# A selective-scan kernel: the list order of layer 1's scans is made again with other durations and priorities

## The chip, the cores and the metric

The kernel runs on one core of one Trainium2 chip. The metric is the device time of one execution in microseconds (us). The core has five engines that run side by side, each working through its own instructions strictly in order: TensorE (PE in the profile; its weight loads are listed apart as PEld), VectorE (DVE), ScalarE (ACT), GpSimd (POOL) and SyncE (SP), which here only issues DMAs. An instruction that must wait for another engine holds up everything behind it on its own engine.

## The reference, cut to what matters

Two layers follow each other. Layer 0 works on four images of 128x128 positions and 192 channels. Layer 1, which the change touches, runs a selective scan in four directions over the same positions, with 16 states for each channel:

```python
proj = einsum('kbcl,kcd->kbld', xs, x_proj_w)          # dpart (12), B (16), C (16)
delta = softplus(einsum('kblr,krc->kblc', dpart, dt_w) + 2 * dt_b)
def step(state, inp):
    d, b, c, uu = inp
    dA = exp(d[..., None] * A_neg)                     # A_neg = -exp(A_logs)
    state = dA * state + (d * uu)[..., None] * b[:, :, None, :]
    y = einsum('kbcn,kbn->kbc', state, c)
    return state, y
```

The four directions' y, plus Ds * xs, are added; a layer norm, a gate and an output projection follow, outside of the change.

## The kernel before, in words

The stages run one after the other: transposing the input, layer 0, layer 1's projection and convolution (in_conv), layer 1's scans (scans), and the outputs. Only the scans are changed. All data is float32.

**Tiling.** The four images make two pairs, and two pairs times four directions times 16 chunks of 1024 positions make 128 steps. In a step lie 6 tiles, each of 64 channels of one image. A tile's 128 partitions hold 64 channels times two halves of the 16 states, so that it takes 8 units, one for each state of a half. Below, "tile 3" is the fourth of its step, and a "unit" is one state pair of a tile. For each unit:

- ACT makes dA = exp(delta * A) into one of two PSUM buffers (exp, L1201).
- DVE scans over 1024 positions, in place in the buffer h (scan, L1207).
- POOL multiplies by C into one of three buffers hc (product, L1213).
- PE sums the two state halves into Y (sum, L1221, two matmuls of 512 columns).

What the scan of a tile starts from is delta * u * B, spread over 8 slots of h. It comes from 8 fills: PE multiplies transposed delta*u by diagonals that carry B (fill, L1174: 8 matmuls on 32-row tiles) into the single PSUM buffer f, and ACT copies it into h (evict, L1185). Each of a tile's 8 evictions writes into all 8 of its slots. So a tile's first scan needs all 8 fills, and there are as many fills as units: 48 in a step. h has 18 slots, so a tile's first eviction waits until the sixth unit of the tile two before it is through its product.

After a tile's 8 sums, DVE adds Y to what earlier directions left (add, L1243, L1247 or L1249, by the direction). Y has one PSUM buffer, so the next tile's first sum waits for this add.

**Preparation of the next step.** While a step's tiles 3 to 5 run, the next step is prepared, and every part of it goes through one PSUM bank, s: two projections (L1028, three matmuls each, copied by ACT, L1034); six step-size matmuls (L1051), each followed by a softplus on ACT (L1054); delta*u on POOL (L1061, three in a step); six groups of four transposes (L1070), copied by ACT or DVE (L1076); eight diagonal matmuls (L1094), each spread by DVE (L1100). As the bank is single, a preparing matmul waits for the engine that empties the bank from the one before. Softplus and exp need different ACT tables: each change between them is an ACT_TABLE_LOAD.

**What sets the order.** Nothing above is emitted where it is written. op() records an operation with its engine, an assumed duration in us, what it reads and writes, and a priority: its place in the list less `early`. Order.emit() then plays the list through: it takes, of all operations whose inputs and buffers are free, the one with the smallest key. The key is the engine's free time for all operations that could start within `idle` of it, and then the priority; a change of ACT table adds `keep` to the rank. What comes out is one fixed instruction order for each engine, the DMA queue of SP among them. The durations decide the order, and nothing else: on the chip the semaphores make each instruction wait for what it really needs.

Of the kernel before, what the change touches and what calls it, by code (L numbers as in the profile page):

```python
# [12 lines left out]
ALU = mybir.AluOpType  # L13
# [187 lines left out]
class Maker:  # L201
# [741 lines left out]
    def scans(self, xc, delta, cs, y, w, ident, alog, dsum, dtb2):  # L943
# [10 lines left out]
        nc, tc = self.nc, self.tc  # L954
# [11 lines left out]
        with ExitStack() as ctx:  # L966
# [9 lines left out]
            for q in (2, 3):  # L976
                nc.vector.tensor_tensor(mask, mask, ident[:, 32 * q : 32 * q + 32], ALU.add)

            od = Order(window=3000, keep=1047, idle=0.500, rate=265e3)
            op = od.op  # L980

            def buf(tag, bufs, *shape, pool=p1, stream=None):
# [5 lines left out]
            us, pj, wts, dT, D, C, dd, h, st, prev, Y = ({} for _ in range(11))  # L988
# [15 lines left out]
            def load_u(s):  # L1004
                p, k, at, j = steps[s]
                for i in range(3):
                    t = us[s, i] = buf("u", 3, 128, T)
                    op("SP", 0.1, lambda t=t, i=i: nc.sync.dma_start(
                        t(), xc[k // 2][p][i][:, j * T : (j + 1) * T]
                    ), writes=[t], size=524e3, early=192)  # L1010
                if at == 0:
                    wt = buf("w", 2, 128, 2, 3, 128)
                    op("SP", 0.2, lambda: [
                        nc.sync.dma_start(wt()[:, 0], w["xp1"][:, k]),
                        nc.sync.dma_start(wt()[:, 1], w["dtw1"][:, k]),
                    ], writes=[wt], size=393e3, early=90)
                    wts[p, k] = wt

            def project(s):
                p, k, _, j = steps[s]  # L1020
                wt, uu = wts[p, k], [us[s, i] for i in range(3)]
                t = pj[s] = buf("pj", 1, 128, T)
                for c in range(2):
                    g = bank("P")

                    def mm(g=g, c=c):
                        for i in range(3):
                            nc.tensor.matmul(  # L1028
                                g(), wt()[:, 0, i], uu[i]()[:, 512 * c : 512 * c + 512],
                                start=(i == 0), stop=(i == 2),  # L1030
                            )

                    op("PE", 2.65, mm, reads=[wt, *uu], writes=[g], claims=[t])
                    op("ACT", 0.59, lambda g=g, c=c: nc.scalar.copy(  # L1034
                        t()[:, 512 * c : 512 * c + 512], g()), reads=[g, t], writes=[(t, c)])

                def store():
                    for e in range(2):
                        r = 64 * e + DR + NS
                        nc.sync.dma_start(cs[2 * p + e][k][:, j * T : (j + 1) * T], t()[r : r + NS])  # L1040

                op("SP", 0.2, store, reads=[(t, 0), (t, 1), t], writes=[("cs", s)], size=131e3)

            def step_sizes(s, i):

                p, k, _, j = steps[s]
                wt, u, x = wts[p, k], us[s, i], pj[s]
                l = buf("l", 3, 128, T)
                for c in range(2):
                    g = bank("P")  # L1050
                    op("PE", 0.9, lambda g=g, c=c: nc.tensor.matmul(  # L1051
                        g(), wt()[:, 1, i], x()[:, 512 * c : 512 * c + 512], start=True, stop=True,
                    ), reads=[wt, (x, c), x], writes=[g], claims=[l], early=-123)
                    op("ACT", 0.6, lambda g=g, c=c: nc.scalar.activation(  # L1054
                        l()[:, 512 * c : 512 * c + 512], g(), AF.Softplus,
                        bias=dtb2[:, i % 2, k : k + 1],
                    ), reads=[g], writes=[l], table="softplus")
                op("SP", 0.1, lambda: nc.sync.dma_start(
                    delta[p][i][k][:, j * T : (j + 1) * T], l()
                ), reads=[l], writes=[("delta", s, i)], size=524e3)  # L1060
                op("POOL", 2.4, lambda: nc.gpsimd.tensor_tensor(u(), l(), u(), ALU.mult),  # L1061
                   reads=[l], writes=[u], early=30)
                t = dT[s, i] = buf("dT", 4, 128, 2, 8, 64)
                for c in range(2):
                    g = bank("P")

                    def mm(g=g, c=c):
                        for q in range(4):
                            b = 512 * c + 128 * q
                            nc.tensor.transpose(  # L1070
                                g()[:, 128 * q : 128 * q + 128], u()[:, b : b + 128], ident
                            )

                    op("PE", 0.95, mm, reads=[u], writes=[g], claims=[t], early=-249)
                    def turn(copy, g=g, c=c):
                        copy(  # L1076
                            t()[:, :, 4 * c : 4 * c + 4],
                            g().rearrange("t (q h c) -> t h q c", h=2, c=64),
                        )

                    if i < 2:
                        op("ACT", 0.6, lambda turn=turn: turn(nc.scalar.copy), reads=[g], writes=[t], early=-579)
                    else:
                        op("DVE", 0.69, lambda turn=turn: turn(nc.vector.tensor_copy),
                           reads=[g], writes=[t], early=-180)

            def diagonals(s, e, sb):
                x, t, g = pj[s], buf("D", 5, 128, 2, 512), bank("D")
                r = 64 * e + DR

                def mm():
                    for a in range(2):
                        b = 256 * sb + 128 * a
                        nc.tensor.matmul(  # L1094
                            g()[:, NS * a : NS * a + NS], x()[:, b : b + 128], ident[:, r : r + NS],
                            start=True, stop=True,
                        )

                def spread():
                    nc.vector.tensor_tensor(  # L1100
                        t().rearrange("t a (n s) -> t (a n) s", s=32),
                        g()[:, : 2 * NS].unsqueeze(2).to_broadcast([128, 2 * NS, 32]),
                        mask.unsqueeze(1).to_broadcast([128, 2 * NS, 32]),
                        ALU.mult,
                    )

                op("PE", 0.4, mm, reads=[(x, sb // 2), x], writes=[g], claims=[t], early=-105)
                op("DVE", 1.2, spread, reads=[g], writes=[t], early=15)
                D[s, e, sb] = t


# [48 lines left out]
            def fill(m, sb, rp):  # L1160

                s, x = divmod(m, 6)
# [3 lines left out]
                td, tD = dT[s, i], D[s, e, sb]  # L1166
                gs = buf("f", 1, 128, 2, 512, pool=psF)
# [10 lines left out]
                                    start=True, stop=True,  # L1178
                                )

                op("PE", 1.12, mm, reads=[td, tD], writes=[gs], claims=h[m])

                def evict():
                    for at, q, nq in runs(m):
# [4 lines left out]
                            gs().rearrange("p n (a q s) -> p q a n s", a=2, s=32)[:, q : q + nq],  # L1189
                        )  # L1190

                op("ACT", 1.13, evict, reads=[gs], writes=h[m])

            def unit(m, q):
                p, k, at, j, x, e, hf, i, r = info(m)
                hq, d, tC = h[m][q], dd[m], C[m // 3, q]
                hs = H[:, (NQ * m + q) % SLOTS]
                a, t = buf("dA", 2, 128, T, pool=psA), buf("hc", 3, 128, T)
                c = (hf * 4 + k) * NQ + q
                way = slice(None) if k % 2 == 0 else slice(None, None, -1)  # L1200
                op("ACT", 1.16, lambda: nc.scalar.activation(  # L1201
                    a(), d(), AF.Exp, scale=alog[:, c : c + 1]),
                    reads=[d], writes=[a], table="exp", early=-522)
                s0 = st.get((x, m - 6))

                def scan():
# [2 lines left out]
                        0.0 if at == 0 else s0()[:, q : q + 1], ALU.mult, ALU.add,  # L1209
                    )  # L1210

                op("DVE", 2.34, scan, reads=[a, *([s0] if at else [])], writes=[hq])
                op("POOL", 2.4, lambda: nc.gpsimd.tensor_tensor(t(), hs, tC(), ALU.mult),  # L1213
                   reads=[hq, tC], writes=[t])
                if q == 0:
                    Y[m] = buf("Y", 1, 128, 512, pool=psY)
                ym = Y[m]
# [5 lines left out]
                            start=(q == 0), stop=(q == NQ - 1),  # L1223
                        )

                op("PE", 0.95, sum_n, reads=[t], writes=[ym], early=-252)

            def finish(m):
                p, k, at, j, x, e, hf, i, r = info(m)
                ym, t = Y[m], buf("y", 2, 128, 512)  # L1230
                if at < NCH - 1:
                    sm = st[x, m] = buf(f"st{x}", 2, 128, NQ)
                    last = T - 1 if k % 2 == 0 else 0

                    def keep():
                        for a, q, nq in runs(m):
                            nc.scalar.copy(sm()[:, q : q + nq], H[:, a : a + nq, last])  # L1237

                    op("ACT", 0.22, keep, reads=h[m], writes=[sm])

                def add():
                    if k == 0:
# [9 lines left out]
                    for th, a in enumerate(y_part(y[k // 2][p][i], m)):  # L1252
                        nc.sync.dma_start(a, t()[64 * th : 64 * th + 64])

                op("DVE", 0.72, add, reads=[ym, *([prev[m]] if k != 2 else [])], writes=[t])
                op("SP", 0.2, store, reads=[t], writes=[("y", p, k // 2, j, x)], size=262e3)

            FILLS = [(sb, rp) for sb in range(4) for rp in range(2)]
# [403 lines left out]
```

## Time and profile before

| | us |
|---|---|
| median of 3 runs | 26409.49 |
| lowest and highest run | 26333.76 and 26457.49 |
| the profiled execution | 26512.26 |
| its span, first to last instruction | 26510.5 |
| of it, the scans (first to last eviction and product), 7180 to 24910 | 17730 |
| PE busy in the scans | 16270.53 |
| DVE busy in the scans | 15700.51 |
| POOL busy in the scans | 15212.16 |
| ACT busy in the scans | 14689.00 |
| granted TensorE clock in the scans | 0.94 |

The profiled execution is 102.8 us (0.4%) above the median of the runs, and some 2 us longer than its span. A busy share is the time in which at least one instruction of an engine was running. The granted clock is the share of full speed that TensorE was given: 1.00 is full, and 0.94 a mean over stretches at full and at half speed. In the waits view a row names the engine and line that waited, whom for, the total, how often, and the longest. In the timeline a bracket at the end of a row gives the idle time of the engine before the instruction and what ended it.

### The profile page before, as it was taken

The numbers are of one execution on the slowest core, as the hardware profiler recorded it, in microseconds if no ns is written. First come the engines' busy times: TensorE is split into PE (matmuls) and PEld (weight loads), VectorE is DVE, ScalarE is ACT, GpSimd is POOL, SyncE is SP. The second block draws the span as 40 slices with busy tenths as digits, with TensorE's granted clock in tenths as the row PEclk, the third lists the DMA queues.
The fourth block names the chain that finished last, engine by engine and source line by source line (L and its number), as shares of the span: only waits on it lengthen the run. The fifth ranks groups of instructions, "written<-read, shape, count | busy, mean of one in ns | idle before, by whom it ended". The sixth has DMA issues, their size and how long they took to land.

```text
span 26510.5 us, 438073 instructions
## 1 busy us (share of the span) xinstructions
PE 24193.3 (91%) x169220; PEld 9017.9 (34%) x169220; DVE 21935.4 (83%) x15401; ACT 21016.8 (79%) x24359; POOL 19902.8 (75%) x9450
## 2 busy tenths in 40 slices
PE   5999999998799999999999999999999999999699
PEld 3333333332233333333333333333333333333255
DVE  4888888888788889989898888888898888988643
ACT  5988898985588888888888888888888888888433
POOL 3777777763488888888888888888888888888400
PEclk7999999998899999999999899999899999999799
DMA  7999999995544444444444444444444444444573
GB/s 213 242 239 241 242 239 241 239 241 182 185 130 127 133 130 136 135 128 125 117 126 134 126 135 130 130 130 130 125 136 131 117 123 115 133 130 130 182 236 105
DMA packets 1667058, 4220.17 MB, mean 159 GB/s; under 512 B 238545, under 2 KB 387473, under 8 KB 1661905
## 3 DMA queue, kind: packets, MB, share of 16 engines
q1 hardware_dynamic: 1664976, 4192.14, 58.0%
q8 instruction: 1340, 21.95, 0.4%
q14 instruction: 742, 6.07, 0.1%
HBM read 3252.11 MB, written 939.10 MB: 158 GB/s over the span
## 4 chain that ended last, share of the span: by engine, by line
PE 40%; DVE 18%; ACT 11%; issue 6%; DMA 4%; POOL 3%; SPq 0%; DVEq 0%; POOLq 0%; ACTq 0%
DVE h L1207 14%; PE f L1174 13%; PE Y L1221 11%; ACT h L1185 6%; PE s L1028 3%; ACT dA L1201 3%; POOL hc L1213 2%; PE s L1051 2%; DMA C<-cs 2%; PE z L785 1%; PE hf L574 1%; DVE D L1100 1%; DVE acc L896 1%; PE f L785 1%; PE s L1094 1%
## 5 line engine op out<-in xcount | busy, mean ns | idle before, releaser
L1213 POOL TENSOR_TENSOR hc<-h,C 128x1024 f32<-128x1024 f32 x6144 | 14335.4, 2362 | 2412.5 <-PE Y L1221 1154.9
L1207 DVE TENSOR_TENSOR_SCAN h<-dA,st,h 128x1024 f32<-128x1024 f32 x5760 | 13130.9, 2331 | 779.9 <-ACT st L1237 290.6
L1185 ACT COPY h<-f 128x1024 f32<-128x1024 f32 (+3 forms) x8192 | 6332.9, 799 | 2256.1 <-PE f L1174 2185.0
L1174 PE MATMUL f<-D,dT 32*64 32x256 f32 x98304 | 7167.9, 408 | 777.5 <-ACT h L1185 633.6
L1221 PE MATMUL Y<-hc,sel 128*64 128x512 f32 x24576 | 7001.5, 657 | 475.1 <-POOL hc L1213 219.9
L1201 ACT ACTIVATE dA<-d,alog 128x1024 f32<-128x1024 f32 x6144 | 6905.9, 1124 | 301.6 <-DVE h L1207 247.2
L1174 PEld LDWEIGHTS f<-D,dT 32*64 32x64 f32 x98304 | 3279.1, 138 | 6688.2 <-ACT h L1185 4815.8
L452 POOL TENSOR_TENSOR xs<-xs,pr 128x1024 f32<-128x1024 f32 x1536 | 3637.3, 2371 | 329.2 <-ACT pr L447 249.4
L595 DVE SCALAR_TENSOR_TENSOR hf<-hh,vec,hf 128x512 f32<-128x512 f32 x3072 | 2317.8, 755 | 412.9 <-PE hf L574 272.7
L1221 PEld LDWEIGHTS Y<-hc,sel 128*64 128x64 f32 x24576 | 1322.6, 141 | 2979.6 <-issue 1811.3
L574 PE MATMUL hf<-sa,diag 96*32 96x512 f32 x18432 | 2152.3, 600 | 13.2 <-DMA sa<-hpad 11.3
L447 ACT ACTIVATE pr<-xi,vec 128x1024 f32<-128x1024 f32 x1536 | 1713.8, 1143 | 301.1 <-POOL xs L452 296.0
L1100 DVE TENSOR_TENSOR D<-s,mask 128x1024 f32<-128x1024 f32 x1024 | 1238.3, 1209 | 842.0 <-PE s L1094 842.0
L534 POOL TENSOR_TENSOR dl<-dl,xs 128x1024 f32<-128x1024 f32 x192 | 454.7, 2368 | 830.6 <-ACT dA L532 735.5
L574 PEld LDWEIGHTS hf<-sa,diag 96*32 96x32 f32 x18432 | 561.9, 109 | 1479.3 <-issue 1390.5
L1061 POOL TENSOR_TENSOR u<-l,u 128x1024 f32<-128x1024 f32 x384 | 907.2, 2363 | 163.4 <-ACT l L1054 136.0
L1207 DVE TENSOR_TENSOR_SCAN h<-dA,h 128x1024 f32<-128x1024 f32 x384 | 857.1, 2274 | 78.5 <-ACT dA L1201 45.3
L1051 PE MATMUL s<-pj,w 128*128 128x512 f32 x1536 | 892.3, 664 | 7.0 <-ACT l L1054 2.8
L1028 PE MATMUL s<-u,w 128*128 128x512 f32 x1536 | 756.4, 630 | 53.3 <-DMA prev<-xc 52.6
L1054 ACT ACTIVATE l<-s,vec 128x512 f32<-128x512 f32 x768 | 527.8, 687 | 328.5 <-PE s L1051 323.9
L1094 PEld LDWEIGHTS s<-ident,pj 128*128 128x128 f32 x4096 | 554.1, 196 | 599.5 <-issue 256.7
L392 PE MATMUL f<-xa,w 96*128 96x512 f32 (+1 forms) x1536 | 724.8, 616 | 25.7 <-ACT xi L407 25.5
(202 smaller groups left out, 21859.5 us busy)
## 6 DMA issues: line engine op xcount, KB each, us to landing
C<-cs SPq DMA_DIRECT2D x4096, 256.0 KB, 4.7
sa<-hpad SPq DMA_DIRECT2D x2304, 276.0 KB, 7.1
d<-delta SPq DMA_DIRECT2D x1536, 256.0 KB, 4.1
u<-xc SPq DMA_DIRECT2D x384, 512.0 KB, 4.6
delta<-l SPq DMA_DIRECT2D x384, 512.0 KB, 3.6
y<-y SPq DMA_DIRECT2D x1536, 128.0 KB, 3.2
hh<-hpad SPq DMA_DIRECT2D x384, 414.0 KB, 7.7
hpad<-hp SPq DMA_DIRECT2D x192, 552.0 KB, 7.2
```

Source lines behind the costliest of these rows:

```text
L447: op("ACT", 1.1, lambda pr=pr, t=t: nc.scalar.activation(rows(pr()), x()[:, t // 3 : t // 3 + R, t % 3 : t % 3 + W], AF.Copy, scale=v(k, V ...
L452: op("POOL", 2.38, lambda pr=pr: nc.gpsimd.tensor_tensor(o(), o(), pr(), ALU.add), reads=[pr], writes=[o], early=-429)
L574: nc.tensor.matmul(o()[32 * g : 32 * g + 32], diag[:, d, s, k, g], x[:, g, :, c0 : c0 + W], start=(d == 0 and s == 0), stop=(d == 1 and s ...
L595: nc.vector.scalar_tensor_tensor(o3, hh()[:, 1 + dy : 5 + dy, PAD + dx : PAD + dx + W], v(k, V0_K + col), o3, ALU.mult, ALU.add,)
L1028: nc.tensor.matmul(g(), wt()[:, 0, i], uu[i]()[:, 512 * c : 512 * c + 512], start=(i == 0), stop=(i == 2),)
L1100: nc.vector.tensor_tensor(t().rearrange("t a (n s) -> t (a n) s", s=32), g()[:, : 2 * NS].unsqueeze(2).to_broadcast([128, 2 * NS, 32]), ma ...
L1174: nc.tensor.matmul(gs()[64 * jn : 64 * jn + 64, n, 256 * a : 256 * a + 256], td()[rt, r // 64, 2 * sb + a], tD()[rt, a, 256 * jn : 256 * j ...
L1185: nc.scalar.copy(H[:, at : at + nq, 256 * sb : 256 * sb + 256].rearrange("p q (a r s) -> p q a r s", a=2, s=32)[:, :, :, 2 * rp : 2 * rp + 2],
L1201: op("ACT", 1.16, lambda: nc.scalar.activation(a(), d(), AF.Exp, scale=alog[:, c : c + 1]), reads=[d], writes=[a], table="exp", early=-522)
L1207: nc.vector.tensor_tensor_scan(hs[:, way], a()[:, way], hs[:, way], 0.0 if at == 0 else s0()[:, q : q + 1], ALU.mult, ALU.add,)
L1213: op("POOL", 2.4, lambda: nc.gpsimd.tensor_tensor(t(), hs, tC(), ALU.mult), reads=[hq, tC], writes=[t])
L1221: nc.tensor.matmul(ym()[64 * th : 64 * th + 64], sel, t()[:, 512 * th : 512 * th + 512], start=(q == 0), stop=(q == NQ - 1),)
```

## The change

No operation is added or removed. The list of 49,432 operations of the scans, what each reads and writes, and all buffers are the same; the assumed durations, the priorities and three settings of the planner differ, and with them the order of the instructions. The diff, without its context:

```diff
-            od = Order(window=3000, keep=1047, idle=0.500, rate=265e3)
+            od = Order(window=3000, keep=937, idle=0.400, rate=265e3)
 # load_u: u, weights
-                    ), writes=[t], size=524e3, early=192)
+                    ), writes=[t], size=524e3)
-                    ], writes=[wt], size=393e3, early=90)
+                    ], writes=[wt], size=393e3)
 # project
-                    op("PE", 2.65, mm, reads=[wt, *uu], writes=[g], claims=[t])
+                    op("PE", 2.65, mm, reads=[wt, *uu], writes=[g], claims=[t], early=-219)
-                        t()[:, 512 * c : 512 * c + 512], g()), reads=[g, t], writes=[(t, c)])
+                        t()[:, 512 * c : 512 * c + 512], g()), reads=[g, t], writes=[(t, c)], early=96)
 # step_sizes: matmul, softplus, delta*u, transposes, copies by ACT and by DVE
-                    op("PE", 0.9, lambda g=g, c=c: nc.tensor.matmul(
+                    op("PE", 1.1, lambda g=g, c=c: nc.tensor.matmul(
-                    ), reads=[wt, (x, c), x], writes=[g], claims=[l], early=-123)
-                    op("ACT", 0.6, lambda g=g, c=c: nc.scalar.activation(
+                    ), reads=[wt, (x, c), x], writes=[g], claims=[l])
+                    op("ACT", 0.69, lambda g=g, c=c: nc.scalar.activation(
-                op("POOL", 2.4, lambda: nc.gpsimd.tensor_tensor(u(), l(), u(), ALU.mult),
-                   reads=[l], writes=[u], early=30)
+                op("POOL", 2.38, lambda: nc.gpsimd.tensor_tensor(u(), l(), u(), ALU.mult),
+                   reads=[l], writes=[u])
-                    op("PE", 0.95, mm, reads=[u], writes=[g], claims=[t], early=-249)
+                    op("PE", 1.16, mm, reads=[u], writes=[g], claims=[t], early=-201)
-                        op("ACT", 0.6, lambda turn=turn: turn(nc.scalar.copy), reads=[g], writes=[t], early=-579)
+                        op("ACT", 0.6, lambda turn=turn: turn(nc.scalar.copy), reads=[g], writes=[t], early=9)
-                           reads=[g], writes=[t], early=-180)
+                           reads=[g], writes=[t], early=-96)
 # diagonals: matmul, spread
-                op("PE", 0.4, mm, reads=[(x, sb // 2), x], writes=[g], claims=[t], early=-105)
-                op("DVE", 1.2, spread, reads=[g], writes=[t], early=15)
+                op("PE", 0.4, mm, reads=[(x, sb // 2), x], writes=[g], claims=[t], early=-180)
+                op("DVE", 1.2, spread, reads=[g], writes=[t], early=930)
 # fill, evict
-                op("PE", 1.12, mm, reads=[td, tD], writes=[gs], claims=h[m])
+                op("PE", 1.1, mm, reads=[td, tD], writes=[gs], claims=h[m])
-                op("ACT", 1.13, evict, reads=[gs], writes=h[m])
+                op("ACT", 1.05, evict, reads=[gs], writes=h[m], early=1074)
 # unit: exp, scan, product, sum
-                op("ACT", 1.16, lambda: nc.scalar.activation(
+                op("ACT", 1.13, lambda: nc.scalar.activation(
-                    reads=[d], writes=[a], table="exp", early=-522)
+                    reads=[d], writes=[a], table="exp", early=75)
-                op("DVE", 2.34, scan, reads=[a, *([s0] if at else [])], writes=[hq])
-                op("POOL", 2.4, lambda: nc.gpsimd.tensor_tensor(t(), hs, tC(), ALU.mult),
+                op("DVE", 2.34, scan, reads=[a, *([s0] if at else [])], writes=[hq], early=57)
+                op("POOL", 2.37, lambda: nc.gpsimd.tensor_tensor(t(), hs, tC(), ALU.mult),
-                op("PE", 0.95, sum_n, reads=[t], writes=[ym], early=-252)
+                op("PE", 1.09, sum_n, reads=[t], writes=[ym], early=-306)
 # finish: keep, add
-                    op("ACT", 0.22, keep, reads=h[m], writes=[sm])
+                    op("ACT", 0.22, keep, reads=h[m], writes=[sm], early=249)
-                op("DVE", 0.72, add, reads=[ym, *([prev[m]] if k != 2 else [])], writes=[t])
+                op("DVE", 0.72, add, reads=[ym, *([prev[m]] if k != 2 else [])], writes=[t], early=567)
```

What this does to the order shows best on one step in the middle. Below, F is a fill, Y a sum, S a scan; dg and D are a diagonal matmul and its spread, mm a step-size matmul, pj a projection, tr four transposes, cp a copy of them by DVE; F4.3 is the fourth fill of tile 4. PE, from the first sum of tile 1 to the first of tile 3, before and after:

```
before  Y1.0 F2.4 Y1.1 F2.5 Y1.2 F2.6 Y1.3 F2.7 Y1.4 Y1.5 F3.0 dg Y1.6 F3.1 Y1.7 F3.2 Y2.0 F3.3 dg
        Y2.1 F3.4 Y2.2 F3.5 pj F3.6 pj F3.7 mm Y2.3 F4.0 Y2.4 Y2.5 mm F4.1 Y2.6 dg Y2.7 tr F4.2 Y3.0
after   Y1.0 F2.3 dg Y1.1 F2.4 Y1.2 F2.5 dg F2.6 Y1.3 F2.7 Y1.4 pj Y1.5 pj F3.0 Y1.6 F3.1 Y1.7 F3.2
        Y2.0 F3.3 mm Y2.1 F3.4 Y2.2 F3.5 Y2.3 F3.6 Y2.4 F3.7 Y2.5 Y2.6 F4.0 mm F4.1 Y2.7 dg Y3.0 F4.2
```

DVE over the whole step, where add4 is the add that ends tile 4, "add5-" that of the step before, and dots stand for the scans between:

```
before  S0.0 S0.1 add5- D S0.2 S0.3 cp S0.4 cp S0.5 ... S1.2 add0 S1.3 ... S1.7 D S2.0 S2.1 add1 D S2.2
        S2.3 D S2.4 ... S3.1 D add2 S3.2 ... S4.3 add3 S4.4 S4.5 D S4.6 S4.7 D S5.0 S5.1 add4 S5.2 S5.3 D
after   S0.0 cp S0.1 add5- S0.2 ... S1.1 D add0 S1.2 D S1.3 S1.4 D S1.5 ... S2.2 add1 S2.3 ... S3.1 add2
        D S3.2 ... S4.1 add3 S4.2 S4.3 S4.4 D D S4.5 ... S5.1 D add4 D S5.2 ... S5.7 cp
```

Over the whole list: on PE, two fills stand directly behind each other 122 times before and 2 times after. Changes of the ACT table number 764 in both orders. Tile 3's and tile 5's last eviction stands on ACT just behind its own first exp before, and behind its second exp after; that of tile 2 stands ahead of the last exp of tile 1 after. POOL's third delta*u of a step stands behind the first product of the next step's tile 0 before, and behind the first product of tile 5 after.

## The prediction, made before the changed kernel ran

> **What bounds the kernel now.** I read the stages first: the scans hold 17730 of 26510.5 us and alone change, and in them no engine is full (PE 92%, DVE 89%, POOL 86%, ACT 83%). So I cut them into their 128 steps by the products on POOL and asked for busy time and clock of each step. Four of them (stretch, its length, busy us and count of PE, PEld, DVE, ACT, POOL, then clock, DMA share, GB/s):
>
> ```profile
> 12724.17:12856.03 131.86, 119.41 (x1042) 44.94 (x1040) 122.39 (x65) 114.76 (x131) 118.77 (x52) 1.00 0.45 123
> 12856.03:12990.62 134.59, 122.50 (x1042) 45.69 (x1040) 122.56 (x65) 115.56 (x139) 118.87 (x52) 0.97 0.45 123
> 14219.17:14357.81 138.64, 127.15 (x1042) 46.68 (x1040) 122.86 (x65) 114.80 (x147) 118.94 (x52) 0.94 0.48 132
> 14623.25:14786.17 162.92, 154.63 (x1042) 54.24 (x1040) 123.94 (x65) 114.31 (x147) 118.99 (x53) 0.76 0.40 113
> ```
>
> The same instructions take 131.9 us at full clock and 162.9 at 0.76, and only PE's busy time grows. Of steps 3 to 126, 53 had a clock of at least 0.98 and took 131.6 us in the mean; 42 at 0.94 to 0.98 took 136.9, 8 at 0.90 to 0.94 took 139.7, 21 below 0.86 took 156.1. The mean is 138.1. So the time has two parts: **131.6 us of work and waits at full clock, and 6.5 us a step, 830 us in all, for TensorE at half speed.**
>
> Next, what comes before half speed. Its stretches last 3.41 us or multiples (6.8, 17.1, 44.4, 51.2, 78.5), so I stepped through in 3.41 us. Three stretches that end where half speed begins, and the one that follows the first:
>
> ```profile
> 14245.34:14248.75 3.41, 2.22 (x34) 0.98 (x28) 3.41 (x3) 2.87 (x5) 3.41 (x2) 1.00 0.00 0
> 14248.75:14265.82 17.07, 17.07 (x86) 4.83 (x84) 13.15 (x7) 10.41 (x16) 10.92 (x6) 0.50 0.23 63
> ...
> 12948.28:12951.69 3.41, 1.91 (x20) 0.74 (x20) 3.41 (x3) 3.20 (x5) 3.38 (x2) 1.00 0.00 0
> ...
> 14627.63:14631.05 3.42, 2.22 (x24) 0.97 (x22) 2.99 (x3) 3.22 (x4) 3.32 (x2) 1.00 1.01 302
> ```
>
> PE was idle for 1.2 to 1.5 of 3.41 us. Of all such stretches at full clock, half speed followed 9 of 9 with PE busy about 1.8 us, 10 of 20 at 2.0, 47 of 135 at 2.2, 15 of 932 from 2.4 to 2.8, and none of 3270 above. **A gap of some 1.2 us on PE inside one such stretch is what costs.** The timeline names three places, with these gaps:
>
> ```profile
> 14247.33 0.45 PE L1174 MATMUL f<-D,dT 32*64 32x256 f32 x4 [1.19 <-ACT h L1185]
> ...
> 12950.88 1.22 PE L1221 MATMUL Y<-hc,sel 128*64 128x512 f32 x4 [1.42 <-DVE y L1247]
> ...
> 14628.69 0.55 PE L1070 MATMUL s<-ident,u 128*128 128x128 f32 x3 [0.63 <-POOL u L1061]
> ```
>
> A: two fills in a row in tile 1, the second waiting for the first's eviction. B: tile 4's first sum waits for the add that empties Y. C: the transposes at the start of tile 0 wait for delta*u; gaps of 0.28 on either side join the 0.63. Over 123 steps A came 33 times (29 of 17 us, +6.9 each against clean steps, 4 of 44 us, +18.5: 274 us), B 24 times (+3.2: 77), C 17 times (51 or 79 us, ten at +20, seven at +31: 420), others 19 times (50). The sum, 821 us, agrees with 123 x 6.5 = 800.
>
> Last, where a clean step loses. DVE is its fullest engine: 122.4 busy of 131.6, idle 9.2. The waits view, from 8000 to 24000 us (115.6 steps, slow ones too):
>
> ```profile
> POOL hc L1213 <- PE Y L1221: 1010.9, 558, 10.0
> DVE D L1100 <- PE s L1094: 734.9, 358, 4.8
> DVE h L1207 <- ACT st L1237: 277.4, 216, 3.5
> DVE h L1207 <- ACT dA L1201: 243.5, 268, 2.7
> ```
>
> The spreads waiting for their diagonals cost 6.4 us a step; POOL waits because sums come late behind the two projections.
>
> **Part by part.** Nothing is added, and table loads (764 x 1.283 us) stay. I walked the new order by hand through a middle step, with durations from the rows: scan 2.33, product 2.36, exp 1.12, eviction 1.02, fill 1.09, sum 1.08, spread 1.21, add 0.67, softplus 0.69, table load 1.28, projection 3.0, step-size matmul 1.07, transposes 0.66, diagonals 0.62.
>
> *The pair of fills (A).* A sum (1.08) now stands between, hiding the 1.02 of eviction. That sum waits for add0, now behind S1.1 and one spread: ready 1.21 + 0.67 = 1.9 after S1.1. The fill before it ends at about 1.5. The gap falls from 1.19 to 0.4, at worst 0.9. From the shares above I take half speed in 7% of steps instead of 27%: 0.07 x 8.3 = 0.6 us a step.
>
> *Adds sooner (B).* Add3 moves from behind S4.3 to behind S4.1, two scans or 4.7 us sooner, so Y4.0 loses its 1.42. Late next is the step-size matmul two places on: table load and softplus end 3.6 us after S4.2, PE has finished Y4.1 at 2.65, gap 0.95. 8% x 3.2 = 0.3 us.
>
> *Third delta\*u (C).* It goes behind P5.0, a fill now stands before its transposes, and by the walk these find it done 2.0 us earlier. C goes: 0.
>
> *New gaps.* In tile 0 a copy and an add follow S0.0 and S0.1. They delay two exps, with them evictions and fills: gaps of 0.55 and 0.85, with 2.15 of work between. A stretch of 3.41 holds 1.26 of them at most, over few alignments: 5% x 25 us (what C costs) = 1.2. Others 0.2. **Clock cost: 0.6 + 0.3 + 1.2 + 0.2 = 2.3 instead of 6.5, or -4.2 us a step.**
>
> *Projections sooner.* They now stand around Y1.5. The longest time without a sum falls from 10.3 us (two projections 6.0, three fills 3.3, a step-size matmul) to 4.1 (one projection, one fill), which three hc buffers cover. This takes away most of POOL's wait and of the spread waits in tile 3.
>
> *Evictions later.* The last evictions of tiles 3 and 5 stand behind the second exp. That exp needs a dA buffer, free only when the last scan of the tile before ends; then 1.12 + 1.02 + 0.1 follow before S3.0 or S5.0 can start. Certain idle time on DVE: 2 x 2.25 = 4.5 a step. On ACT a small copy and, in tile 5, a softplus queue behind the waiting exp; PE's next fill waits for the eviction, but two sums stand ahead of it and cover that.
>
> *Spreads close to their diagonals.* D and D in tile 4 follow each other through the one bank: the second waits 0.7. The first waits 1.3 behind softplus, a third 0.35; two adds wait 0.75 and 0.65 for sums; other places give 0.8. In all the walk finds 9.0 us of idle DVE, against 9.2 now: the waits change place, and a clean step stays at 131.4. Bounds: the certain waits alone (5.2) give -4.0; every spread waiting as the closest one does now (1.37 a step, measured at tile 0's) gives 8 x 1.37 + 4.5 + 1.75 = 17.2, or +8.0. I take the walk's -0.2, as it has the waits in order.
>
> *DMA queue.* SP's moves cost nothing: the third store of delta, which waits for the last softplus, goes ahead of the next C loads. These have until P0.0, 21 us after that softplus by the walk, against 4.7 us to landing. If that cover went, each late load would stop POOL for its remainder. Projections wait for inputs loaded about four tiles earlier.
>
> **Sum.** 128 x (-4.2 - 0.2) = -563 us against the profile's 26512, or 25949. That run is 103 above the median, so I take the difference from the median: 26409 - 563 = 25846, rounded to **25850**.
>
> [...] The stretches above show half speed after 1.2 us idle in 3.41. [...]
>
> **Rivals.** *Slower.* The gaps in tile 0 line up in more stretches than 5%. Once slow there, PE stays so until the projections, as with C: 25 us each. At a share of 5% + 4.4/25 = 23% of steps the gain is gone; at 50% the step costs +6.9, or 27290. For it: the threshold is a knife edge (135 stretches at 2.2). Against it: a single gap stays below 1.2. 13%. *No change.* A and B stay as gaps of over 1.2 in their new places (B at its step-size matmul in 75% of steps: 2.4 us; A as now 2.2; tile 0 1.2): clock 6.0, -90 us, 26320. 13%. *Much faster.* DVE's waits shrink to the certain 5.2 and the clock term to about 2: 128 x (-4.0 - 4.5) = -1090, or 25320. For it: projections and adds free PE and POOL ahead of where I wait. 15%. *It does not do what it says:* the durations hardly matter. The order shows otherwise on PE and DVE, so this falls under no change.
>
> **How the numbers follow.** The likeliest case has 59%, from 25600 to 26150 by itself. The range 25450 to 26420 reaches into both other cases. A measurement of this kernel can tell 0.5% (132 us) from no change: faster 0.74, same 0.13, slower 0.13.
>
> **What would show it.** Right: scans' clock from 0.94 to about 0.98; most steps near 131; no wait of transposes for delta*u; POOL's wait for sums at a third; DVE waiting for evictions 4.5 a step. Wrong: clock 0.94 or less with half speed starting in tile 0; or steps at full clock away from 131.4, which fails the walk.

## The result, and the profile after

| | before | after |
|---|---|---|
| median of 4 runs, us | 26433.49 | 26123.53 |
| lowest and highest | 26333.76 and 26474.52 | 26120.49 and 26164.81 |
| the profiled execution | 26512.26 | 26164.81 |
| steps 3 to 126, counted from 0: mean length, us | 137.9 | 135.1 |
| of them, steps without half speed: number, mean length, us | 50, 131.5 | 43, 132.1 |
| starts of half speed in these steps, and time at half speed | 92, 1949 us | 98, 836 us |

By the medians the changed kernel takes 310 us (1.2%) less, where 563 (2.1%) were forecast; the recorded ratio of the runs is 0.9897 (95% interval 0.9868 to 0.9925), or 1.0% less. The direction was right, and the time lies inside the range; the gain is about half of the sum. The two profiles differ by 347 us, and so do steps 3 to 126 (17095.9 against 16749.0).

First the page of after, with the shares of the span, the granted clock in slices, and the scan and the fill:

```profile
PE 23774.6 (91%) x169220; PEld 8894.1 (34%) x169220; DVE 21933.6 (84%) x15401; ACT 21066.2 (81%) x24359; POOL 19914.6 (76%) x9450
...
PEclk7999999999889999999999999999999999999799
...
L1207 DVE TENSOR_TENSOR_SCAN h<-dA,st,h 128x1024 f32<-128x1024 f32 x5760 | 13113.5, 2333 | 757.9 <-ACT h L1185 362.0
L1174 PE MATMUL f<-D,dT 32*64 32x256 f32 x98304 | 6879.5, 395 | 1082.5 <-ACT h L1185 885.9
```

The page alone misleads here. PE is as full as before (91%), and the clock row shows 9 in nearly every slice. But 9 stands for anything from 0.90 up, and the clock of the whole scans (7228 to 24562 us) is 0.97. So the steps again, cut by the products on POOL (stretch, length, busy us and count of PE, PEld, DVE, ACT, POOL, then clock, DMA share, GB/s): one clean step and the two kinds that make up most of the rest.

```profile
12665.64:12797.74 132.10, 120.10 (x1052) 44.98 (x1044) 122.60 (x65) 114.79 (x132) 118.89 (x52) 1.00 0.48 126
12797.74:12932.80 135.06, 123.25 (x1048) 45.69 (x1040) 122.70 (x65) 114.91 (x138) 118.86 (x51) 0.97 0.45 121
14286.47:14423.23 136.76, 124.97 (x1052) 46.20 (x1044) 122.77 (x65) 114.52 (x132) 119.05 (x52) 0.96 0.48 132
```

The steps of 150 to 163 us are gone. In their place a majority of steps lost a little: 78 of 124 had a clock between 0.94 and 0.98. Half speed starts as often as before, but it lasts mostly 6.8 or 10.2 us and at most 27.3, no longer up to 78.5.

The waits view of after, from 8000 to 24000 us (engine, line, whom for, total, times, longest):

```profile
PE f L1174 <- ACT h L1185: 825.8, 2345, 1.0
...
DVE D L1100 <- PE s L1094: 433.2, 473, 3.7
...
DVE h L1207 <- ACT h L1185: 363.5, 199, 3.8
...
POOL hc L1213 <- PE Y L1221: 244.7, 224, 5.2
...
DVE h L1207 <- ACT st L1237: 196.8, 154, 2.2
```

POOL's wait for sums is a quarter of the 1010.9 before, the spreads' wait for diagonals fell from 734.9 to 433.2, and the scans now wait more for evictions. Before, that row was:

```profile
DVE h L1207 <- ACT h L1185: 161.4, 124, 3.5
```

Last, the place where half speed starts now: the middle of tile 1, in 80 of 123 steps (steps 2 to 124; so are all counts by place below). Four stretches, and the timeline of PE between them (start, duration, engine, line, out<-in; in the bracket the idle time before it):

```profile
12823.34:12826.75 3.41, 3.35 (x29) 1.08 (x32) 3.32 (x2) 2.62 (x3) 2.05 (x1) 1.00 0.00 0
12826.75:12830.16 3.41, 2.55 (x38) 1.42 (x35) 3.41 (x3) 3.03 (x3) 3.07 (x2) 1.00 0.00 0
12830.16:12836.99 6.83, 6.83 (x26) 1.98 (x27) 5.40 (x4) 4.02 (x5) 5.87 (x3) 0.50 0.01 2
12836.99:12840.40 3.41, 3.41 (x11) 1.12 (x10) 3.41 (x2) 1.30 (x3) 2.05 (x2) 1.00 0.58 154
```

```profile
12825.45 1.08 PE L1221 MATMUL Y<-hc,sel 128*64 128x512 f32 x4
12826.56 1.09 PE L1174 MATMUL f<-D,dT 32*64 32x256 f32 x16
12827.58 0.62 PE L1094 MATMUL s<-ident,pj 128*128 128x16 f32 x4
12829.07 1.09 PE L1174 MATMUL f<-D,dT 32*64 32x256 f32 x16 [0.86 <-ACT h L1185]
12830.09 1.94 PE L1221 MATMUL Y<-hc,sel 128*64 128x512 f32 x4
```

This is "F2.5 dg F2.6" of the order: a fill, a diagonal matmul of 0.62, and the next fill, which waits 0.86 for the eviction of the first. PE is idle for 0.86 of 3.41 us and busy for 2.55. Before, 15 of 932 stretches with 2.4 to 2.8 us of busy PE led to half speed; now it is 96 of some 970, and 80 of them lie at this one place. The sum that follows, at 12830.09, already takes 1.94 instead of 1.08.

The other 16 starts have the same shape, with the four transposes between two fills: 14 at the start of tile 0, for 3.41 us each, and two in tile 3, for 23.9 and 27.3 us. One in tile 0, at 13331.92:

```profile
13329.83 0.66 PE L1070 MATMUL s<-ident,u 128*128 128x128 f32 x4
13331.12 1.25 PE L1174 MATMUL f<-D,dT 32*64 32x256 f32 x16 [0.63 <-ACT h L1185]
```

The order has fill, diagonals, fill once in each of the 123 steps, and before the change nowhere. With transposes between the fills, where the gap is 0.59 in the mean, it led to half speed in these 16 of 485 cases.

### The profile page after: what moved, and what is told of

Its sections match the earlier page's. It is cut to its first block, busy times and chain, and to the rows that moved or that the text cites. A ratio compares the mean times of both kernels' runs of the same rounds, so it can differ in the third digit from the quotient of the medians.

```text
span 26162.7 us, 437897 instructions
## 1 busy us (share of the span) xinstructions
PE 23774.6 (91%) x169220; PEld 8894.1 (34%) x169220; DVE 21933.6 (84%) x15401; ACT 21066.2 (81%) x24359; POOL 19914.6 (76%) x9450
## 4 chain that ended last, share of the span: by engine, by line
PE 33%; ACT 20%; DVE 17%; issue 7%; DMA 3%; POOL 1%; SPq 0%; DVEq 0%; ACTq 0%; POOLq 0%
DVE h L1207 13%; PE f L1174 12%; ACT h L1185 11%; ACT dA L1201 5%; PE Y L1221 5%; PE s L1028 3%; PE s L1051 2%; DVE D L1100 2%; PE z L785 1%; PE s L1094 1%; PE hf L574 1%; ACT L1054 1%; ACT l L1054 1%; DVE acc L896 1%; PE f L785 1%
## 5 line engine op out<-in xcount | busy, mean ns | idle before, releaser
L1174 PE MATMUL f<-D,dT 32*64 32x256 f32 x98304 | 6879.5, 395 | 1082.5 <-ACT h L1185 885.9
L1221 PE MATMUL Y<-hc,sel 128*64 128x512 f32 x24576 | 6767.8, 635 | 141.2 <-DVE y L1249 49.1
L1174 PEld LDWEIGHTS f<-D,dT 32*64 32x64 f32 x98304 | 3183.9, 133 | 6837.0 <-ACT h L1185 5673.3
L1028 PE MATMUL s<-u,w 128*128 128x512 f32 x1536 | 829.1, 681 | 53.4 <-DMA prev<-xc 52.7
L660 PE MATMUL g<-xz,w 96*128 96x512 f32 x1536 | 730.3, 611 | 21.8 <-DVE y L653 21.7
```

The lines of the kernel that those rows point to most:

```text
L1028: nc.tensor.matmul(g(), wt()[:, 0, i], uu[i]()[:, 512 * c : 512 * c + 512], start=(i == 0), stop=(i == 2),)
L1174: nc.tensor.matmul(gs()[64 * jn : 64 * jn + 64, n, 256 * a : 256 * a + 256], td()[rt, r // 64, 2 * sb + a], tD()[rt, a, 256 * jn : 256 * j ...
L1221: nc.tensor.matmul(ym()[64 * th : 64 * th + 64], sel, t()[:, 512 * th : 512 * th + 512], start=(q == 0), stop=(q == NQ - 1),)
```

## The experiments

Two theories were set against each other. **G, gaps alone** (the prediction's): idle time of PE in a stretch of 3.41 us decides. **K, kind of work:** what PE does in the stretch counts too; a fill, whose matmuls start four at a time (in after within 0.02 us of each other, on 64 of 128 rows together), counts less than a sum on 128 rows, and a matmul of 16 columns hardly at all. K came from a fit to 8953 stretches of the two profiles above, an estimate: in units of a sum's time, a step-size matmul weighs 1.04, transposes 0.66, a fill 0.58, a diagonal matmul 0.21, and half speed follows where a stretch holds less than 1.61 us so weighted. On the stretches that it was fitted to, it calls 177 of the 189 starts, with 186 called in all; the experiments are its test.

In the added code below, lines behind the edit are moved: by 8 in the runs with added matmuls, by 13 in the third.

### 1 and 2: two matmuls added at the new place, on 128 rows or on 32

```diff
 # diagonals, behind the two matmuls of 16 columns
+                    if e == 1 and sb == 3:
+                        b = 256 * sb
+                        c = 512 * (sb // 2)
+                        for _ in range(2):
+                            nc.tensor.matmul(
+                                g()[:, 32:512], x()[:128, b : b + 128], x()[:128, c : c + 480],
+                                start=True, stop=True,
+                            )
 # the second experiment: x()[:32, ...] in both operands instead of x()[:128, ...]
```

> The changed kernel, and in each step two more matmuls of 480 columns on all 128 rows, straight behind the diagonal matmul of tile 1 that stands between two fills; they write into unused columns of the same bank, and nothing reads them. Theory K (the kind of work counts): half speed follows a stretch of 3.41 us whose PE work, weighted by kind, is too small; a logistic fit over both traces gives weight 1 to sums and step-size matmuls, 0.58 to fills, 0.66 to transposes, 0.2 to diagonals, and a threshold of 1.6 us. The stretches in tile 1 hold about 1.9 us of fill and 0.6 of diagonals, weighted 1.25; 1.0 us more at weight 1 lifts them to 2.3. Half speed in tile 1 goes from 65% of steps to under 5%, the mean step from 135.0 to about 132.5, the median from 26124 to 25800 (25750 to 25860). Rival G (only idle time of PE counts): the added work fills the 0.86 us gap, so the same result here; the two part at the next kernel. Rival N (half speed has nothing to do with what stands there): no change, 26120 to 26160.

> The same two added matmuls of 480 columns at the same place, but on 32 of the 128 rows, so that they take PE about as long. Theory K, if the weight goes by the rows in use (a fill uses 64 of 128 at a time, weight 0.58; a sum all 128, weight 1): they add 0.25 us weighted, 1.25 to 1.5, still below 1.6. Half speed in tile 1 stays in 35 to 65% of steps, and the median lies at 26000 to 26130. Rival G (idle time alone): as with all rows, under 5% of steps, 25750 to 25860.

Measured on 128 rows: 25904.01 us, ratio to before 0.979 (0.9756 to 0.9824); half speed starts in tile 1 in 0 of 123 steps. On 32 rows: 26155.07, ratio 0.9888 (0.9853 to 0.9922); half speed starts there in 52 of 123. Both orders are the same, PE is about as busy (14663 and 14682 of 16000 us), clean steps are alike (132.8 and 132.9), and yet the two are 251 us apart. The second run, its windows and the timeline ahead of the first start:

```profile
12784.17:12787.58 3.41, 3.36 (x27) 1.69 (x24) 3.13 (x2) 2.79 (x4) 2.36 (x2) 1.00 0.02 5
12787.58:12797.82 10.24, 10.24 (x44) 3.02 (x43) 6.97 (x4) 4.95 (x5) 6.94 (x3) 0.50 0.01 2
12924.12:12927.53 3.41, 3.41 (x32) 1.70 (x25) 2.47 (x2) 3.15 (x4) 3.37 (x2) 1.00 0.00 0
12927.53:12937.77 10.24, 10.24 (x40) 3.17 (x33) 8.39 (x5) 4.20 (x6) 6.45 (x4) 0.50 0.17 44
```

```profile
12784.70 1.09 PE L1182 MATMUL f<-D,dT 32*64 32x256 f32 x16
12785.73 0.62 PE L1094 MATMUL s<-ident,pj 128*128 128x16 f32 x4
12786.27 2.31 PE L1102 MATMUL s<-pj 32*128 32x480 f32 x4
12788.51 1.98 PE L1182 MATMUL f<-D,dT 32*64 32x256 f32 x16
```

PE was busy for 3.36 and 3.41 of 3.41 us, and half speed followed (clock 0.50 for 10.24 us both times). That ends G. The times missed K's ranges by a little: the first lies 44 us above its 25860 at most, since the two matmuls outlast the gap and the spread behind them waits 0.82 a step; the second lies 25 us above its 26130.

### 3: the last evictions of tiles 3 and 5 ahead of the second exp

The order of after, with one exchange in each of these tiles. It was to show what the step "Evictions later" costs.

```diff
 # at the end of the planner, for the scans only; the lists evict, exp and place, and the upkeep of place, are left out here
+        for m in range(6, len(exp) // 8):
+            last, second = evict[8 * m + 7], exp[8 * m + 1]
+            if place[second] < place[last]:
+                i, j = place[second], place[last]
+                order[i : j + 1] = order[i + 1 : j + 1] + [second]
```

> The changed kernel with one swap on ACT: the last eviction of tiles 3 and 5 stands ahead of the second exp of its tile again. My prediction named this place as a certain loss of 4.5 us a step. If the place costs it (P): the waits before the first scans of tiles 3 and 5 (2.35 and 1.98 us in the changed kernel) fall to below 0.5 each, the step gains 3 to 4 us, the median falls to 25600 to 25750. If the fill before the eviction is late anyway, as my walk had it (fill of tile 3 ends 0.3 us before the exp would, that of tile 5 0.5 us), only 0.3 to 0.8 us a step: 26020 to 26090 (L).

Measured: 28310.88 us, ratio 1.0694 (1.0649 to 1.0739). Both expectations missed. The two steps of it that stayed at full clock took 132.4 us. S3.0 waited 2.42 in them, as in the same two steps of after, so the exchange gave nothing there. The last eviction, now ahead of the second exp, waits for its fill instead, as the second expectation had it; that fill has waited for the eviction before it, through the single buffer f:

```profile
26070.76 1.01 ACT L1198 COPY h<-f 128x1024 f32<-128x1024 f32 x1 [1.02 <-PE f L1187]
26071.87 2.35 DVE L1220 TENSOR_TENSOR_SCAN h<-dA,st,h 128x1024 f32<-128x1024 f32 x1 [2.42 <-ACT h L1198]
```

Of tile 5 these two steps tell nothing: S5.0 waits at most 0.17 in them in both kernels. For the rest, half speed starts at the beginning of tile 5 (90 times) and of tile 3 (37 times) and lasts 37 to 96 us; the place in tile 1 stays (59 times). One in tile 5, and the timeline around its start:

```profile
16265.30:16268.71 3.41, 3.41 (x26) 1.08 (x25) 2.51 (x2) 2.16 (x4) 3.41 (x2) 1.00 0.95 285
16268.71:16272.12 3.41, 1.97 (x20) 0.81 (x18) 3.41 (x2) 3.38 (x5) 2.68 (x2) 1.00 0.03 10
16272.12:16313.08 40.96, 40.65 (x214) 14.07 (x212) 24.42 (x16) 21.91 (x26) 23.98 (x11) 0.50 0.55 154
16313.08:16316.49 3.41, 3.21 (x32) 0.91 (x24) 3.41 (x2) 2.76 (x5) 1.50 (x1) 1.00 0.55 154
```

```profile
16269.03 1.09 PE L1187 MATMUL f<-D,dT 32*64 32x256 f32 x16
16271.56 1.56 PE L1064 MATMUL s<-pj,w 128*128 128x512 f32 x2 [1.44 <-ACT l L1067]
16273.05 1.98 PE L1187 MATMUL f<-D,dT 32*64 32x256 f32 x16
```

A step-size matmul now waits 1.44 us for the softplus ahead of it. PE is then 99% busy for 41 us with the clock at 0.50. In 81 of the 90 cases half speed ends in tile 0 of the next step, in a stretch mostly of sums; in the other 9 it lasts 95.6 us, to the projections in tile 1.

### 4 and 6: the change in two parts

Of the planner's settings two differ, `keep` and `idle`, and not three. The fourth experiment has those of before, the sixth those of after.

```diff
 # 4, durations only: the code of before with after's durations, for example
-                op("ACT", 1.13, evict, reads=[gs], writes=h[m])
+                op("ACT", 1.05, evict, reads=[gs], writes=h[m])
 # 6, priorities only: the code of after with before's durations, for example
-                op("ACT", 1.05, evict, reads=[gs], writes=h[m], early=1074)
+                op("ACT", 1.13, evict, reads=[gs], writes=h[m], early=1074)
```

> The kernel before with the new assumed durations alone; priorities and planner settings as before. If the durations make the gain (D): 26120, as the changed kernel. If a retuned set of priorities makes it (R): no gain. In its order two fills follow each other directly 361 times instead of 122 (2 in the changed kernel), three times a step, each with a gap of about 1.1 us; by theory K at least one more place with half speed a step at 3 to 7 us: slower than before, 26600 to 27000.

> The changed kernel's priorities and planner settings with the durations of before; nothing of the computation is changed. With durations alone (the fourth experiment) it was 27783. R (durations and priorities fit only each other): the order this makes puts four sums in a row in tile 5 and one projection among fills, so new gaps come: 26400 to 27200, clock below 0.95. Rival P (the priorities do the work, and durations read in a trace are a detail): 26050 to 26250, the same clock as the changed kernel, 0.96.

Measured: durations only 27782.99 us, ratio 1.0498 (1.0462 to 1.0534); priorities only 27867.13, ratio 1.0538 (1.0501 to 1.0574). R had the sign right in both and the size too small by 667 us or more. From 8000 to 24000 us the two profiles show, in this order:

```profile
8000.00:24000.00 16000.00, 14281.13 (x112264) 5176.11 (x112264) 13313.85 (x6909) 12458.28 (x14854) 12824.69 (x5506) 0.91 0.44 119
```

```profile
8000.00:24000.00 16000.00, 14606.03 (x110810) 5338.09 (x110806) 13157.26 (x6816) 12308.43 (x14722) 12678.92 (x5434) 0.87 0.43 118
```

The clock is 0.91 and 0.87, against 0.98 for after in the same stretch. With priorities only, half speed starts in tile 1 (75 times), in tile 4 (43) and at the last unit of tile 5 (44, of which 37 last 68 to 75 us); its 5 steps without half speed take 133.4. With durations only it starts 289 times, 146 of them in tile 0, and the two steps without it take 136.2, so that there the order loses time at full clock too. So neither part works alone. That the durations came from a trace is not what gains: with the old priorities they lose 5%.

### 5: one added matmul instead of two

> After the change with one added matmul, instead of the two of the first experiment, on 128 rows and 480 columns behind the last diagonals of tile 1; its result is never read and nothing is left out. One matmul lasts some 0.5 us, which leaves about 0.35 of the 0.86 us of idle PE at the new place. K (the clock goes by the kind of work in a 3.41 us stretch, as well as by idle time): half speed in tile 1 in fewer than 10% of steps, and the spread that waits for the added matmul waits 0.4 us less than with two: clean steps 132.4 us, and 25904 less 128 x 0.4 = 25850 (25800 to 25900). Rival E (one matmul is too little, and two only just sufficed): half speed in tile 1 stays in 20 to 60% of steps, and the time is 26000 to 26120.

The edit of experiment 1 with `range(1)`. Measured: 25797.79 us, ratio to before 0.9766 (0.9741 to 0.9791), 2 us below the least that K gave. Half speed starts in tile 1 in 0 of 123 steps. A clean step, and the timeline at the place:

```profile
12524.55:12656.58 132.03, 120.94 (x1054) 45.20 (x1046) 122.66 (x65) 114.63 (x132) 118.75 (x51) 1.00 0.46 125
```

```profile
12553.47 1.09 PE L1182 MATMUL f<-D,dT 32*64 32x256 f32 x16
12554.49 0.62 PE L1094 MATMUL s<-ident,pj 128*128 128x16 f32 x4
12554.96 1.05 PE L1102 MATMUL s<-pj 128*128 128x480 f32 x2
12555.97 1.09 PE L1182 MATMUL f<-D,dT 32*64 32x256 f32 x16
```

The matmul takes 1.05 us where 0.5 was assumed, and fills the gap to the end. The spread behind it waits 0.02 a step, so the added work is free: 108 steps without half speed take 132.1, as in after. This is the fastest of the kernels run here, and what sets it apart from after is the clock (0.976 against 0.961 in the profiled executions). The starts behind transposes stay (10 in tile 0, 4 in tile 3).

### 7: patterns on TensorE by themselves

Ahead of the scans, PE alone runs one pattern after another, with 20 sums between them. A gap is made by a DVE copy that rewrites the matmuls' input. The code in short:

```diff
+                for n in range(50): pfill(0)          # fills, two row tiles of 32 rows at a time
+                for n in range(200): rows(128, 16)    # 128 rows, 16 columns
+                for k in (128, 96, 64, 32):
+                    for n in range(60): rows(k, 512)
+                # 12 times: gap, two sums; 12 times: gap, two fills (a short and a longer gap each)
+                # from half speed (gaps and 16-column matmuls): 30 sums; 30 fills; sums and fills
+                # in turn; sums and pairs of rows(64, 512) in turn
```

> The changed kernel, with TensorE patterns alone run ahead of the scans and never read (nothing is left out); some 1.2 ms longer, and only its clock by pattern counts. Between the patterns stand 20 sums (21 us) at 128 rows. K, by the weights fitted to the scans (a stretch of 3.41 us triggers half speed below 1.61 us of weighted work: sum 1, fill 0.58, 16-column matmul 0.2): fills without a gap stay at full clock, 16-column matmuls without a gap run at half, 128 and 96 rows without a gap stay full, 32 rows half, 64 rows at the edge; two sums and a gap of 0.4 or 1 us stay full; two fills and a gap of 1 us run at half. From half speed, sums alone return to full within 7 us, fills alone stay at half for as long as they last (30 fills, 33 us at full speed), sums and fills in turn stay for 10 us or more. G (idle time alone): everything without a gap stays at full clock, whatever its rows and columns; gaps act alike for sums and fills; from half speed all continuous patterns return within 7 us.

One execution was taken. Its windows, inside the patterns: fills; 16 columns; 64 rows; 32 rows; sums with a gap; fills with a gap; then, entered at half speed, sums (two windows); fills; sums and fills in turn; sums and matmuls on 64 rows in turn (stretch, length, PE busy and count, clock, DMA share, GB/s):

```profile
7165.00:7205.00 40.00, 40.00 (x748) 1.00 0.01 2
7231.00:7303.00 72.00, 72.00 (x339) 0.50 0.00 0
...
7463.00:7511.00 48.00, 48.00 (x113) 1.00 0.00 0
7537.00:7629.00 92.00, 92.00 (x109) 0.50 0.00 0
...
7696.00:7721.00 25.00, 19.04 (x82) 1.00 0.00 1
...
7752.00:7780.00 28.00, 25.92 (x232) 0.50 0.00 1
...
7871.00:7874.00 3.00, 3.00 (x10) 0.50 0.00 0
7876.00:7887.00 11.00, 11.00 (x54) 1.00 0.01 1
7922.00:7969.00 47.00, 47.00 (x444) 0.50 0.01 1
7996.00:8048.00 52.00, 52.00 (x274) 0.50 0.00 1
8079.00:8154.00 75.00, 75.00 (x109) 0.50 0.00 0
```

Two of its gaps, behind sums and behind fills:

```profile
7697.26 1.94 PE L981 MATMUL yy<-X,selp 128*64 128x512 f32 x8 [0.60 <-DVE X L998]
...
7744.25 1.96 PE L988 MATMUL ff<-X,selp 32*64 32x256 f32 x32 [0.30 <-DVE X L998]
```

The two rows with gaps decide. The short and the longer gap behind sums came out at 0.30 and 0.60 us, those behind fills at 0.30 and 0.39. Sums with a gap of 0.60 after every two left PE busy for 76% of the time, at a clock of 1.00. Fills with a gap of only 0.30 left it busy for 93% (at 0.50; 1.96 of 2.26 us, or 87%, before) and lost the clock. K held in every pattern that it named, and 64 rows, which it had put at the edge, stayed full. Its gap of 1 us behind fills was not made; at 0.30 the last stretch ahead of half speed holds 2.81 us of fills, which its weight makes 1.63, a hair above its estimated limit of 1.61. G fell in six of the ten patterns (16 columns, 32 rows, fills with a gap, and the last three). In the last four patterns more was needed to leave half speed than to keep full speed: sums alone left it after one stretch of 3.41 us, while fills (51 us), sums and fills in turn (57) and sums and 64 rows in turn (81) stayed at half to the end of the pattern, with PE busy for the whole of the windows above.

## Where the prediction was right, and which step failed

The sum was -4.2 us a step for the clock and -0.2 for clean steps. Measured over 124 steps it was 6.4 to 3.0, or -3.4, and +0.6. Of the 216 us that are missing from the profiles' difference (563 less 347), 0.8 x 124 = 99 are the clock, as much again the clean steps, and 18 that the sum counted 128 steps. The medians differ by another 37 less: the profiled execution of before lay 79 above its median of four, that of after 41. So the shortfall has two halves, the clock and the clean steps. And that the clock term came as near as it did, 3.0 us a step instead of 2.3, is luck: 2.1 were set down for places that cost nothing, and 0.2 for those that cost 2.9.

- **A and B: right, and better than forecast.** Taken at 0.6 + 0.3 a step, they cost nothing: half speed starts in neither place. At C the wait for delta*u is gone, as forecast, but the fill that now stands ahead of the transposes brings another: the fill behind them waits some 0.6 us for the eviction. That makes the 14 starts in tile 0, at 1.8 us each 0.2 a step instead of 0.
- **New gaps in tile 0: did not come.** The copy and the add behind S0.0 and S0.1, taken at 1.2 a step, started no half speed; the starts of tile 0 lie ahead of them, at the transposes.
- **"Others 0.2": the step that failed.** The place in tile 1 belongs here, and it costs 33 x 2.8 + 47 x 4.7 = 313 us, or 2.5 a step; the two starts in tile 3 add 0.2. The prediction had treated A as solved because a sum stands between most fills, and it looked for gaps near 1.2 us. But in one place a diagonal matmul of 0.62 stands between two fills instead. Its gap of 0.86 lies below the "gap of some 1.2 us on PE inside one such stretch", and so was given no price. That measure is wrong: in before it sorted the stretches well (9 of 9 at 1.8 us busy), as long gaps and light work came together there. Experiment 2 shows half speed with no gap at all, 5 removes the cost of this place with one matmul on 128 rows, and 7 shows fills losing the clock with a gap of 0.30 us, where sums kept it with 0.60, with nothing else running.
- **How long half speed lasts: misread.** The prediction took it that PE stays slow "until the projections", at 25 us a start in tile 0. Already in before 10 of the 17 starts at C ended ahead of them, after 51 us, in stretches mostly of sums. Counted over the scans of the eight profiles without added patterns: of 3740 stretches at half speed with more than 1.45 us of fills in 3.41 none was the last, and all 978 last ones held less. In after such a stretch is near: the projections (in tile 2 before, in tile 1 now) follow the new place within a few us, and two sums in a row follow that in tile 0. So most starts cost 2 to 5 us and not 25, and as many starts as before cost less than half. In experiment 3 fills and sums alternate behind the start, and half speed lasts 37 us and more.
- **Clean steps: the walk was near, its end on the wrong side.** This is the other half of the shortfall: 132.1 against 131.4. In clean steps the two scans behind late evictions wait 2.3 + 1.9 = 4.2 us (4.5 taken), where before they waited 1.1 + 0.0. The spreads and adds came out as walked but for the first spread of tile 4 (1.8 instead of 1.3) and a spread in tile 1 that the prediction did not name (0.6). DVE's busy time is 0.2 more. The cause given for the late evictions, the second exp, does not hold in tile 3: without it the fill is late there, and the wait stays (2.4 in all steps, with and without the exchange). For tile 5 it is open: the exchange cut that wait from 1.9 to 1.3 in the mean, but nearly all of its steps ran at half speed in part.
- **Projections sooner: right.** POOL's wait for sums fell by 766 us of 16000.
- **DMA queue: nearly free.** POOL's waits that ended with a load of C rose from 0.8 us to 186.7, most of them at tile 3's first product. But the scan that this product needs is late there as well: beyond it the loads add some 25 us in all, 0.2 a step.

Of the rivals, "no change" (26320) and "much faster" (25320) are both further from 26123 than the likeliest case, and "slower" did not come.

## What to carry to other kernels

When TensorE's clock is part of the time, look at what it does in the stretch and not only at whether it is busy: here a fill, a matmul of 16 columns and a wait of 0.86 us lost the clock in 80 of 123 steps, and fills and sums in turn did not win it back in 57 us. Find in a trace both the stretch before half speed and the one that ends it; here the second set the price (17 x 25 us at C before, 80 x 3.9 us at the place in tile 1 after). The gap of 0.86 us was worth one unread matmul on all rows, as the spread behind it then waited only 0.02 us a step: it gained 326 us, about as much as the change itself. And this planner's durations and priorities acted as one setting, as each alone lost 5%: change them together, and judge the order by the clock that it gets.

## What the runs showed of the hardware

- In 7 keeping the clock and winning it back were different conditions. At full clock, fills alone (40 us) and 64 rows alone (48 us) kept it; from half speed, fills alone (51 us), sums with fills (57 us), and sums with 64-row matmuls (81 us) did not win it back; sums did in 3.41 us.
- In 7 fills lost the clock with a gap of 0.30 us after every two, and sums kept it with one of 0.60. Whether it is the rows or the area of the array in use that counts is open. In the trace of after four matmuls of a fill start within 0.02 us of each other (64 rows by 128 columns together), and both matmuls of a sum within 0.01 us. One sum takes 1.08 us at full clock and two in a row 1.94, so the second adds 0.86; one matmul of 512 columns on 128 rows and 128 columns takes 1.13 and three in a row 2.84, so each further one adds 0.86 as well. By this estimate a sum fills the array and a fill half of it, by rows and by area alike. The values that the matmuls carry weren't varied either.
- In 7, 200 matmuls of 16 columns on 128 rows, back to back, ran at a clock of 0.50 for the whole of their window of 72 us, with PE busy throughout.
- All clocks seen in single stretches were 1.00 or 0.50; values between, such as 0.97 for the scans of after, are means.
